# Four graph layers on a sparse matrix: moving a check of the matrix from layer 0 to layer 2, and the transposed writes to another queue

## The chip, the core and the metric

The kernel runs on one core of a Trainium2 chip. The metric is the device time of one execution in microseconds (us). Engines are named as in the profile: PE is the matrix engine (PEld its weight loads), DVE the vector engine, ACT the scalar engine, POOL the general one, SP the engine that here only issues transfers. A name with a q (SPq, ACTq) is an engine's instruction queue where it issues transfers. Each engine takes its instructions in order; engines wait for each other by semaphores.

## The reference

`x` is 2708 x 128 and `adj` 2708 x 2708, mostly zeros (some 16 entries in a row, all positive in the inputs, diagonal included). Four layers follow each other, each on the rectified layer norm `h` of `x`, each added to `x`. Cut to what matters:

```
layer 0:  x += (adj.T @ h) / adj.sum(axis=0)
layer 1:  m[i, j] = gelu(s[i] + d[j] + msg_b)            # s, d: two projections of h
          agg[i] = sum over j of m[i, j] * adj[i, j]
          u = gelu([h, agg] @ upd_w.T + upd_b) + h
          x += layer_norm(u) * ln_w + ln_b
layer 2:  msg = relu((adj @ h) @ W_msg.T + b_msg)
          x += gru_cell(msg, h)
layer 3:  for two heads: softmax over the mask (adj > 0 or diagonal) of
          leaky_relu(s_src[i] + s_dst[j]), times the head's values, + norm, elu
```

## The kernel before, in words

Rows and columns are cut into tiles of 128: 21 whole tiles and a tail of 20 (`NT` = 22, `TAIL` = 20). Six groups of up to four tiles are `GROUPS`: groups 0 to 4 have four tiles, group 5 two, one of them the tail. A chunk of columns is one group wide, up to 512.

**Layer 0** goes over items `(c, s)`: column chunk c of `adj`, row group s. For c from 0 to 4 the items run in order; the last chunk (`LAST` = 5) has its six pieces `z` loaded while c = 3 runs and worked between the items of c = 4. Loads go through SP's queue into `a`, a ring of four buffers (`RING`), so that the load of an item goes out three items ahead. For an item:

- DVE lists the largest eight values of each block of 124 columns in a row and their positions (`list_cut`, lines 348 and 350). Layer 1 works on these lists instead of on the whole matrix. Blocks that hold the diagonal are first copied by POOL with the diagonal taken out (`mask_near`).
- PE transposes the 4 x 4 blocks of the item into `p_T` (two PSUM banks, line 383), ACT copies each bank to `aT` (line 387), and SP writes `aT` to `adjT` in device memory (line 388), for layer 2. Each bank holds four transposes.
- Between the transposes PE multiplies the item with `h0` (line 369), into sums over the rows; a column of ones gives the degree. For c = 0 the products stand after all four transposes, since h0 is still being made by ACT (`sum_rows`, `sum_squares`, `normal_rows`), one group an item.
- ACT takes the sign of the item and adds it up into `total` (line 399, and 403 for the tail), and, where c = s, adds up the diagonal into `own`.

When a chunk's sums are complete, the items of the next chunk carry its further work: `invert` (DVE, s = 0), `spread` (ACT, POOL, s = 1), `sum_rows`, `sum_squares`, `normal_rows`, `turn_rows` (s = 5: PE transposes rows of h to `p_h`, ACT copies to `hT`), and one chunk later `destinations` and `split_destinations`. The order of all instructions is written out by hand (`manual_schedule`).

**Layer 1** opens with a list of single steps for the first row tiles: `count_rows`, `rank`, `select_rows` and so on. Among them stand the lists of the last column chunk, `list_last(n)` for the 22 row tiles, which read `z`. Then 23 periods work through the row tiles, with POOL, DVE and ACT preparing what PE multiplies. At its end DVE compares `total` with the number of listed entries and the signs of the diagonal; a difference, or a list or row that is too full, sets `flag`, and then a second, dense program runs after this one. With the given inputs it does not run.

**Layer 2** goes over six chunks of rows. `aggregate` loads a chunk of `adjT` in five pieces of up to five tiles, each piece to one of three buffers `a2` (SP, line 1247); the last piece has one whole tile and the tail of 20. DVE and POOL derive the mask from a piece (lines 1251 and 1254), PE multiplies it with h into `p_agg` (line 1259). `finish_chunk` is what follows for a chunk; its steps lie between the products of the next chunk, at distances counted in units of PE's work: ACT copies `aggc` and `hc` (1270, 151), PE and ACT make `msg` (1282), the gates (1294, 1295) and `nn`, DVE makes `y`, then come the layer norms for layer 3 (`h` and `z`, both line 136), `z3T` (1336), the `hv` products, `own_e` (1357), PE's `p_row` (1363), `own_T`, and two small transfers from ACT's queue for `row` (1370).

**Layer 3** weighs and multiplies the mask's rows (lines 1090 and 1120). It is not touched.

Of the kernel before, what the change touches and what calls it, by code (L numbers as in the profile page):

```python
# [20 lines left out]
F32 = mybir.dt.float32  # L21
BF16 = mybir.dt.bfloat16
AF = mybir.ActivationFunctionType
ALU = mybir.AluOpType
# [6 lines left out]
P = 128  # L31
# [29 lines left out]
def listed_layers(ctx: ExitStack, tc: tile.TileContext, x, adj, w, out, flag):  # L61
# [79 lines left out]
    def span(t, k):  # L141

        return t * P, min(k * P, N - t * P)
# [12 lines left out]
    val = keep.tile([P, NT, NB, S], F32, name="val")  # L156
    col = keep.tile([P, NT, NB, S], U16, name="col")
    own = keep.tile([P, NT], F32, name="own")
    total = keep.tile([P, len(GROUPS) + 1, len(GROUPS)], F32, name="total")
    nc.gpsimd.memset(total, 0.0)  # L160
    nc.gpsimd.memset(own, 0.0)
    inv = keep.tile([P, NT], F32, name="inv_deg")

# [118 lines left out]
    once0 = l0.enter_context(tc.tile_pool(name="l0h", bufs=1))  # L282
    pool = l0.enter_context(tc.tile_pool(name="l0k", bufs=2))
    marked = l0.enter_context(tc.tile_pool(name="l0n", bufs=8))
    turned = l0.enter_context(tc.tile_pool(name="l0t", bufs=7))
    sump = l0.enter_context(tc.tile_pool(name="l0p", bufs=4, space=PSUM))
    turnp = l0.enter_context(tc.tile_pool(name="l0q", bufs=2, space=PSUM))
    h0 = once0.tile([P, NT, D + 1], F32, name="h0")
# [47 lines left out]
    def list_cut(c, s, n):  # L336
# [9 lines left out]
        for k in range(0, len(units), 2):  # L346
            for b, v in units[k : k + 2]:
                nc.vector.max(val[0:m, n, b, :], v)  # L348
            for b, v in units[k : k + 2]:
                nc.vector.max_index(col[0:m, n, b, :], val[0:m, n, b, :], v)  # L350

    def work_cut(c, s):

        g0, gk = GROUPS[s]
        t0, tk = GROUPS[c]
        i0, iw = span(g0, gk)
        lo = window(c)[0]
        a = cuts[c, s]
        if s == 0:
            accs[c] = [  # L360
                sump.tile([P, CH], F32, name="sums")[:, 0 : 2 * (D + 1)].rearrange("p (q d) -> p q d", q=2)
                for _ in range(0, tk, 2)
            ]

        def products(n):
            m = size(n)
            for q in range(tk):
                k, e = size(t0 + q), (t0 + q) * P - lo
                nc.tensor.matmul(  # L369
                    accs[c][q // 2][0:k, q % 2, :], a[0:m, n - g0, e : e + k], h0[0:m, n, :],  # L370
                    start=(n == 0 and q % 2 == 0), stop=(n == NT - 1), skip_group_check=True,
                )

        todo = list(range(g0, g0 + gk))
        js = list(range(t0, t0 + tk))
        turns = [js[q : q + 2] for q in range(0, tk, 2)] if gk < 4 == tk else [[j] for j in js]
        for js in turns:
            p = turnp.tile([P, CH], F32, name="p_T")
            k, n = size(js[0]), len(js)
            for i, j in enumerate(js):  # L380
                for q in range(gk):
                    m, e = size(g0 + q), j * P - lo
                    nc.tensor.transpose(  # L383
                        p[0:k, i * iw + q * P : i * iw + q * P + m], a[0:m, q, e : e + k], ident[0:m, 0:m]
                    )
            aT = turned.tile([P, CH], F32, name="aT")
            nc.scalar.copy(aT[0:k, 0 : n * iw], p[0:k, 0 : n * iw])  # L387
            nc.sync.dma_start(
                adjT[0:k, js[0] : js[0] + n, i0 : i0 + iw], aT[0:k, 0 : n * iw].rearrange("p (j i) -> p j i", j=n)
            )  # L390
            if c > 0 and todo and gk == 4:
                products(todo.pop(0))
        for n in todo:
            products(n)

        e0, e1 = t0 * P - lo, t0 * P - lo + span(t0, tk)[1]
        whole = gk if gk == 4 else gk - 1
        sign = pool.tile([P, 4, CH], BF16, name="sign")
        nc.scalar.activation(
            sign[:, 0:whole, 0 : e1 - e0], a[:, 0:whole, e0:e1], AF.Sign, accum_out=total[:, s, c : c + 1]  # L400
        )
        if whole < gk:
            nc.scalar.activation(
                sign[0:TAIL, whole, 0 : e1 - e0], a[0:TAIL, whole, e0:e1], AF.Sign,
                accum_out=total[0:TAIL, s + 1, c : c + 1],
            )
# [62 lines left out]
    for i, (c, s) in enumerate(order):  # L469
# [5 lines left out]
            )  # L475
        for n in range(g0 + 1, g0 + gk):
            list_cut(c, s, n)
        if c > 0 and s == 0:
            invert(c - 1)
        if i + 1 < len(order):  # L480
            mask_near(*order[i + 1])
# [8 lines left out]
        if c == 0:  # L490
            for stage, g in (
# [5 lines left out]
                (),  # L497
            )[s]:
                stage(h0, *GROUPS[g]) if stage is normal_rows else stage(*GROUPS[g])
        elif s == 1:  # L500
            spread(c - 1)
        elif s == 2:
            sum_rows(*GROUPS[c - 1])
        elif s == 3:
            sum_squares(*GROUPS[c - 1])
        elif s == 4:
            normal_rows(h, *GROUPS[c - 1])
        elif s == 5:
            turn_rows(c - 1)
        if c > 1 and s == 0:  # L510
            destinations(c - 2)
        if c > 1 and s == 2:
            split_destinations(c - 2)
        if c == LAST - 1 and s > 0:
            work_cut(LAST, s - 1)
# [6 lines left out]
        if (c, s) == (2, 3):  # L522
# [5 lines left out]
            nc.gpsimd.tensor_copy(src_self[:, 0, :], msg_wT[:, 0, :])  # L528
            nc.gpsimd.tensor_tensor(src_self[:, 1, :], msg_wT[:, 0, :], msg_wT[:, 1, :], ALU.add)

    enter(LAST - 1)
    destinations(LAST - 2)
    work_cut(LAST, LAST)
    for q, k in ((0, P), (1, TAIL)):
        nc.scalar.copy(last_sums[0:k, q, :], accs[LAST][0][0:k, q, :])
    for s in range(len(GROUPS)):
# [26 lines left out]
    with (  # L563
# [408 lines left out]
            for k in range(1, GB):  # L972
                put_more(t, k)

        def list_last(n):
            list_cut(LAST, n // 4, n)
# [8 lines left out]

        puts = ExitStack()
        for step, n in (
            (list_last, 0), (count_rows, 0), (rank, 0), (list_last, 1), (select_rows, 0), (describe, 0), (rows, 4),
            (list_last, 2), (list_last, 3), (count_next, 0), (turn_rows, 4), (split_destinations, 3),
            (finish_rows, 0), (fetch_both, 0), (rank, 1), (destinations, 4), (enter, 5), (place, 0), (pass_on, 0),  # L990
            (sources, 0), (select_rows, 1), (split_destinations, 4), (rows, 5), (describe, 1),
            *((list_last, n) for n in range(4, 10)), (columns, 0), (turn_rows, 5), (destinations, 5),
            (finish_rows, 1), (fetch_both, 1), (rank, 2), (split_destinations, 5), (place, 1), (select_rows, 2),
            *((list_last, n) for n in range(10, 16)), (describe, 2), *((list_last, n) for n in range(16, NT)),
            (close_lists, 0),
        ):
            step(n)
# [4 lines left out]
        if True:  # L1002
# [6 lines left out]
        puts.close()  # L1009


        SETS = len(GROUPS) + 1
        lost = fix.tile([P, 4, NT], F32, name="lost1")
        nc.vector.reduce_sum(lost[:, 0, :], rows_n, AX.X)
        nc.vector.tensor_scalar(lost[:, 1, :], own, 0.0, None, ALU.is_gt)
        nc.vector.tensor_scalar(lost[:, 2, :], own, 0.0, None, ALU.is_lt)
        nc.vector.tensor_tensor(lost[:, 0, :], lost[:, 0, :], lost[:, 1, :], ALU.add)
        nc.vector.tensor_tensor(lost[:, 0, :], lost[:, 0, :], lost[:, 2, :], ALU.subtract)
        found, there = lost[:, 1, 0:SETS], lost[:, 2, 0:SETS]
        nc.vector.reduce_sum(  # L1020
            found[:, 0 : SETS - 2], lost[:, 0, 0 : NT - 2].rearrange("p (s t) -> p s t", t=4), AX.X
        )
        nc.vector.tensor_copy(found[:, SETS - 2 : SETS], lost[:, 0, NT - 2 : NT])
        nc.vector.reduce_sum(there, total, AX.X)
        nc.vector.tensor_tensor(there, there, found, ALU.not_equal)
        nc.vector.reduce_sum(flag, there, AX.X)
        over = fix.tile([P, 2], F32, name="over1")
        many = once.tile([P, NT, NB], BF16, tag="picked", name="many")
        nc.vector.tensor_tensor(many, ends, rows_n, ALU.add)
# [4 lines left out]
        for q in range(2):  # L1034
            nc.vector.tensor_tensor(flag, flag, over[:, q : q + 1], ALU.add)
    lists.close()


# [15 lines left out]
    ident_8 = l3.tile([P, P], U8, name="ident_8")  # L1054
    nc.vector.tensor_copy(ident_8, ident)
    PIECE = 5
    RUNS = ((0, 3), (3, 8), (11, 8), (19, 3))
    MOST = 8
    accs = ctx.enter_context(tc.tile_pool(name="l23p", bufs=1, space=PSUM))
# [174 lines left out]
    with (  # L1234
# [6 lines left out]
        def aggregate(t0, k0, pa, j0):  # L1241
# [5 lines left out]
            nc.sync.dma_start(a[:, 0:whole, 0:n], adjT[:, j0 : j0 + whole, c : c + n])  # L1247
            if whole < jn:
                nc.sync.dma_start(a[0:TAIL, whole, 0:n], adjT[0:TAIL, NT - 1, c : c + n])
            most = min(whole, PIECE - 1)  # L1250
            nc.vector.tensor_scalar(mask[:, j0 : j0 + most, c : c + n], a[:, 0:most, 0:n], 0.0, None, ALU.is_gt)
            if most < jn:
# [12 lines left out]
        def finish_chunk(t0, k0, pa):  # L1265
# [95 lines left out]
            yield 2  # L1361
            p = bank("p_row")
            nc.tensor.transpose(p[0 : 2 * k0, 0:P], own_e[:, 0 : 2 * k0], ident)
            turned = zpool.tile([8, P], F32, name="own_T")
            nc.scalar.copy(turned[0 : 2 * k0, :], p[0 : 2 * k0, 0:P])
            passed = wdram.tile([8, P], F32, name="own_d")
            nc.scalar.dma_start(passed[0 : 2 * k0, :], turned[0 : 2 * k0, :])
# [23 lines left out]
    nc.vector.tensor_scalar(wide[:, 1, :], sv, -LIMIT, None, ALU.is_lt)  # L1391
    over = out_pool.tile([P, 1], F32, name="over3")
    nc.vector.reduce_sum(over, wide, AX.XY)
    nc.vector.tensor_tensor(flag, flag, over, ALU.add)

    for q in range(5):
# [477 lines left out]
```

## Time and profile before

| | |
|---|---|
| median of 3 runs | 1079.67 us (1075.68 to 1081.86) |
| profiled execution: its time | 1080.01 us |
| its span | 1078.2 us |
| mean granted PE clock | 0.94 |
| busy PE, PEld, DVE | 934.4, 816.0, 795.4 us |
| busy ACT, POOL | 516.6, 471.0 us |
| moved by DMA | 133.64 MB |

The profile is of one execution. Busy times are sums over the span; stages with different limits lie behind them, so the tables by stretch say more. Issuing a transfer isn't counted as busy. "Idle before" an instruction names what ended the wait; a wait for several semaphores is put down to the one that came last.

### The profile page before, as it was taken

How to read it: one execution, taken by the hardware profiler on the slowest of the kernel's cores; microseconds unless marked ns; L12 is line 12 of the kernel's file. 1: busy time of each engine (PE TensorE's matmuls, PEld its weight loads, DVE VectorE, ACT ScalarE, POOL GpSimd, SP SyncE). 2: the span in 40 equal slices, each digit the busy share in tenths (PEclk: the TensorE clock that was granted, in tenths of full speed). 3: DMA queues.
4: the chain of work that ended last, by engine and by line, in shares of the span. 5: the costliest groups of instructions: out<-in, count | busy, mean ns of one | idle time of the engine just before them, and what ended most of it. 6: DMA issues, size and time to landing. Idle time of an engine off the chain costs nothing. (4 is left out here: it accounts for less than half of the span.)

```text
span 1078.2 us, 23412 instructions
## 1 busy us (share of the span) xinstructions
PE 934.4 (87%) x8632; PEld 816.0 (76%) x8632; DVE 795.4 (74%) x2748; ACT 516.6 (48%) x1427; POOL 471.0 (44%) x596
## 2 busy tenths in 40 slices
PE   3789878893399999999969978999988999999983
PEld 3789778772399999999969943444477899989982
DVE  7789978717877778897848264566668987898693
ACT  5968858664266666676646622333332200240142
POOL 6322221222397777898958354444311210250042
PEclk9899999985599999999989978999989999999996
DMA  8599899622133333333132045666410000000000
GB/s 286 183 337 299 257 364 346 224 91 84 50 100 124 123 119 97 118 98 113 62 108 83 29 147 206 206 224 212 138 37 2 27 9 1 2 16 6 2 11 19
DMA packets 77090, 133.64 MB, mean 124 GB/s; under 512 B 13980, under 2 KB 29456, under 8 KB 76966
## 3 DMA queue, kind: packets, MB, share of 16 engines
q1 hardware_dynamic: 75150, 129.26, 36.1%
q10 hardware_dynamic: 1816, 2.80, 0.8%
q8 instruction: 70, 1.15, 0.4%
q14 instruction: 54, 0.44, 0.1%
HBM read 85.41 MB, written 30.87 MB: 108 GB/s over the span
## 5 line engine op out<-in xcount | busy, mean ns | idle before, releaser
L721 POOL TENSOR_SCALAR put<-count,line,value 128x128 f32<-128x128 f32 x176 | 198.5, 1138 | 44.6 <-DVE value L710 30.7
L1120 PE MATMUL att<-hv,wt 128*128 128x129 f32 x1672 | 194.4, 277 | 8.7 <-DVE wt L1090 8.7
L1120 PEld LDWEIGHTS att<-hv,wt 128*128 128x128 f32 x1672 | 190.8, 193 | 11.6 <-DVE wt L1090 8.6
L807 PE MATMUL p_m<-d,cols 124*128 124x128 bf16 (+1 forms) x1452 | 163.5, 221 | 7.9 <-DVE cols L752 7.9
L803 PE MATMUL p_m<-s,sel 128*128 128x128 bf16 x1452 | 163.0, 221 | 7.4 <-ACT g L815 7.4
L1090 DVE SCALAR_TENSOR_TENSOR wt<-row,lift,mask 128x1024 f32<-128x1024 f32 (+1 forms) x132 | 138.7, 1082 | 23.2 <-PE att L1120 23.2
L120 POOL TENSOR_TENSOR n_r<-n_r,minus_half 128x4 f32<-128x4 f32 (+1 forms) x27 | 39.0, 1446 | 255.6 <-DVE n_r L119 251.9
L828 PE MATMUL agg<-put,g 128*128 128x128 f32 (+1 forms) x968 | 122.5, 278 | 0.0
L1259 PE MATMUL p_agg<-a,hs 128*128 128x512 f32 (+2 forms) x264 | 112.0, 567 | 10.7 <-issue 6.0
L369 PE MATMUL sums<-h,a 128*128 128x129 f32 (+1 forms) x880 | 121.2, 286 | 0.0
L828 PEld LDWEIGHTS agg<-put,g 128*128 128x128 f32 x968 | 113.2, 192 | 0.0
L369 PEld LDWEIGHTS sums<-h,a 128*128 128x128 f32 (+1 forms) x880 | 112.3, 202 | 0.9 <-issue 0.2
L383 PE MATMUL p_T<-ident,a 128*128 128x128 f32 (+1 forms) x440 | 74.1, 291 | 44.3 <-ACT aT L387 38.0
L803 PEld LDWEIGHTS <-sel 128*128 128x128 bf16 x1452 | 104.6, 98 | 9.2 <-issue 8.7
L807 PEld LDWEIGHTS <-cols 124*128 124x128 bf16 (+1 forms) x1452 | 103.8, 99 | 8.2 <-DVE cols L752 8.2
L730 ACT ACTIVATE put<-mine,value 128x128 f32<-128x128 bf16 x308 | 100.5, 391 | 0.0
L815 ACT ACTIVATE g<-p_m 128x512 f32<-128x512 f32 x132 | 72.6, 551 | 54.7 <-PE agg L828 42.3
L383 PEld LDWEIGHTS p_T<-ident,a 128*128 128x128 f32 (+1 forms) x440 | 54.8, 148 | 53.3 <-ACT aT L387 42.2
L1259 PEld LDWEIGHTS p_agg<-a,hs 128*128 128x128 f32 (+1 forms) x264 | 48.6, 198 | 60.9 <-issue 54.1
L350 DVE FIND_INDEX8 col<-val,a 128x8 uint16<-128x124 f32 x342 | 91.6, 279 | 0.0
L387 ACT COPY aT<-p_T 128x512 f32<-128x512 f32 (+2 forms) x122 | 66.1, 563 | 51.4 <-PE p_T L383 31.0
L348 DVE MAX8 val<-a 128x8 f32<-128x124 f32 x342 | 78.9, 271 | 10.5 <-DMA a<-in_adj 10.5
(282 smaller groups left out, 1559.8 us busy)
## 6 DMA issues: line engine op xcount, KB each, us to landing
adjT<-aT SPq DMA_DIRECT2D x105, 256.0 KB
a<-adjT SPq DMA_DIRECT2D x20, 1280.0 KB
spread<-passed SPq DMA_DIRECT2D x22, 704.0 KB
later<-sel SPq DMA_DIRECT2D x22, 616.0 KB
a<-in_adj SPq DMA_DIRECT2D x5, 1152.0 KB
a<-in_adj SPq DMA_DIRECT2D x5, 1120.0 KB
a<-in_adj SPq DMA_DIRECT2D x5, 1088.0 KB
a<-in_adj SPq DMA_DIRECT2D x5, 1056.0 KB
```

What stands on the lines that cost most here:

```text
L348: nc.vector.max(val[0:m, n, b, :], v)
L350: nc.vector.max_index(col[0:m, n, b, :], val[0:m, n, b, :], v)
L369: nc.tensor.matmul(accs[c][q // 2][0:k, q % 2, :], a[0:m, n - g0, e : e + k], h0[0:m, n, :], start=(n == 0 and q % 2 == 0), stop=(n == NT ...
L383: nc.tensor.transpose(p[0:k, i * iw + q * P : i * iw + q * P + m], a[0:m, q, e : e + k], ident[0:m, 0:m])
L721: nc.gpsimd.tensor_scalar(st["put", 0][:, b, :], count, st["line"][:, b : b + 1], st["value"][:, b : b + 1], ALU.is_equal, ALU.mult,)
L730: nc.scalar.activation(st["put", 1][:, b - HP, :], st["mine"][:, b - HP, :], AF.Identity, scale=st["value"][:, b : b + 1])
L803: nc.tensor.matmul(p[:, b - b0, :], st["sel"][:, b, :], s3[:, q, t % 2, :], start=(q == 0), stop=False)
L807: nc.tensor.matmul(p[:, b - b0, :], st["cols"][0:kb, b, :], d3[0:kb, b, q, :], start=False, stop=(q == 2))
L828: nc.tensor.matmul(agg, g[:, b - 4 * k, :], put, start=(b == 0), stop=False)
L1090: nc.vector.scalar_tensor_tensor(wt[:, 0:n], row[:, k, c : c + n], lift[:, j, k : k + 1], mask[:, j, c : c + n], op0=ALU.max, op1=ALU.mult,)
L1120: nc.tensor.matmul(banks[s // 3][:, s % 3, :], wt[:, q * P : (q + 1) * P], hv[:, j, k, :], start=(v < 2 and s // 3 not in touched), stop=( ...
L1259: nc.tensor.matmul(pa[:, 0:n], h[0:k, j, :], a[0:k, j - j0, 0:n], start=(j == 0), stop=(j == NT - 1))
```

## The change

1. The signs (lines 399 and 403), their sums `total` and the comparison at the end of layer 1 are taken out.
2. In layer 2 ACT adds up the negative parts of each piece of `a2` into `below`, one or two tiles to an instruction; a sum above zero sets `flag`.
3. The writes of `aT` are issued from ACT's queue, each after the next copy. `aT` has eleven buffers instead of seven.
4. For chunks 0 to 2, the work on a chunk's complete sums (`invert`, `spread` and what follows) begins one item later; `turn_rows` moves to s = 0 of the chunk after, `destinations` and `split_destinations` one item on, and for chunk 3 `turn_rows` stands after `enter(4)`.
5. Four `list_last` stand before `enter(4)`; the others close up in layer 1's opening.
6. `own_T` is taken from another pool.

```diff
-    total = keep.tile([P, len(GROUPS) + 1, len(GROUPS)], F32, name="total")
-    nc.gpsimd.memset(total, 0.0)
...
-    turned = l0.enter_context(tc.tile_pool(name="l0t", bufs=7))
+    turned = l0.enter_context(tc.tile_pool(name="l0t", bufs=11))
...
+    written = []
+    def write_one():
+        if written:
+            nc.scalar.dma_start(*written.pop())
...
             nc.scalar.copy(aT[0:k, 0 : n * iw], p[0:k, 0 : n * iw])
-            nc.sync.dma_start(
+            write_one()
+            written.append((
                 adjT[0:k, js[0] : js[0] + n, i0 : i0 + iw], aT[0:k, 0 : n * iw].rearrange("p (j i) -> p j i", j=n)
-            )
+            ))
...
-        nc.scalar.activation(
-            sign[:, 0:whole, 0 : e1 - e0], a[:, 0:whole, e0:e1], AF.Sign, accum_out=total[:, s, c : c + 1]
-        )
...
-        if c > 0 and s == 0:
+        off = 1 if c < LAST - 1 else 0
+        if c > 0 and s == off:
             invert(c - 1)
...
-        elif s == 1:
+        elif s == 1 + off:
             spread(c - 1)
-        elif s == 2:
+        elif s == 2 + off:
             sum_rows(*GROUPS[c - 1])
-        elif s == 3:
+        elif s == 3 + off:
             sum_squares(*GROUPS[c - 1])
-        elif s == 4:
+        elif s == 4 + off:
             normal_rows(h, *GROUPS[c - 1])
-        elif s == 5:
-            turn_rows(c - 1)
         if c > 1 and s == 0:
+            turn_rows(c - 2)
+        if c > 1 and s == 1:
             destinations(c - 2)
-        if c > 1 and s == 2:
+        if c > 1 and s == 3:
             split_destinations(c - 2)
...
+    for n in range(4):
+        list_last(n)
     enter(LAST - 1)
+    turn_rows(LAST - 2)
     destinations(LAST - 2)
     work_cut(LAST, LAST)
+    write_one()
...
-        nc.vector.reduce_sum(there, total, AX.X)
-        nc.vector.tensor_tensor(there, there, found, ALU.not_equal)
-        nc.vector.reduce_sum(flag, there, AX.X)
...
+    below = l3.tile([P, 3 * len(GROUPS) * ((NT + PIECE - 1) // PIECE)], F32, name="below")
+    nc.gpsimd.memset(below, 0.0)
+    looked = []
...
+            for m, q0, q1 in ((P, 0, min(2, whole)), (P, 2, min(4, whole)), (P, 4, whole), (TAIL, whole, jn)):
+                if q1 > q0:
+                    junk = pool.tile([P, 2, CH], U8, name="junk2")
+                    i = len(looked)
+                    looked.append(i)
+                    nc.scalar.activation(
+                        junk[0:m, 0 : q1 - q0, 0:n], a[0:m, q0:q1, 0:n], AF.Relu, scale=-1.0,
+                        accum_out=below[0:m, i : i + 1],
+                    )
...
-            turned = zpool.tile([8, P], F32, name="own_T")
+            turned = pool.tile([8, P], F32, name="own_T")
...
+    nc.vector.tensor_scalar(below, below, 0.0, None, ALU.is_gt)
+    nc.vector.reduce_sum(over, below, AX.X)
     nc.vector.tensor_tensor(flag, flag, over, ALU.add)
```

More of the change, by code (lines that the diff above doesn't have):

```diff
@@ L394, in work_cut @@
             products(n)
[L396 to L399, printed above, removed]
-            sign[:, 0:whole, 0 : e1 - e0], a[:, 0:whole, e0:e1], AF.Sign, accum_out=total[:, s, c : c + 1]
-        )
[L402 to L406, printed above, removed]
         if c == s:
@@ L529, in listed_layers, with list_last @@
             nc.gpsimd.tensor_tensor(src_self[:, 1, :], msg_wT[:, 0, :], msg_wT[:, 1, :], ALU.add)
+    def list_last(n):
+        list_cut(LAST, n // 4, n)
+    for n in range(4):
+        list_last(n)
     enter(LAST - 1)
+    turn_rows(LAST - 2)
     destinations(LAST - 2)
     work_cut(LAST, LAST)
+    write_one()
     for q, k in ((0, P), (1, TAIL)):
@@ L973, in put_rest @@
                 put_more(t, k)
-        def list_last(n):
-            list_cut(LAST, n // 4, n)
         def count_next(_):
@@ L987, in listed_layers @@
         for step, n in (
-            (list_last, 0), (count_rows, 0), (rank, 0), (list_last, 1), (select_rows, 0), (describe, 0), (rows, 4),
-            (list_last, 2), (list_last, 3), (count_next, 0), (turn_rows, 4), (split_destinations, 3),
+            (count_rows, 0), (rank, 0), (list_last, 4), (select_rows, 0), (describe, 0), (rows, 4),
+            (list_last, 5), (list_last, 6), (count_next, 0), (turn_rows, 4), (split_destinations, 3),
             (finish_rows, 0), (fetch_both, 0), (rank, 1), (destinations, 4), (enter, 5), (place, 0), (pass_on, 0),
             (sources, 0), (select_rows, 1), (split_destinations, 4), (rows, 5), (describe, 1),
-            *((list_last, n) for n in range(4, 10)), (columns, 0), (turn_rows, 5), (destinations, 5),
+            *((list_last, n) for n in range(7, 12)), (columns, 0), (turn_rows, 5), (destinations, 5),
             (finish_rows, 1), (fetch_both, 1), (rank, 2), (split_destinations, 5), (place, 1), (select_rows, 2),
-            *((list_last, n) for n in range(10, 16)), (describe, 2), *((list_last, n) for n in range(16, NT)),
+            *((list_last, n) for n in range(12, 17)), (describe, 2), *((list_last, n) for n in range(17, NT)),
             (close_lists, 0),
@@ L1009, in listed_layers @@
         puts.close()
[L1012 to L1023, printed above, removed]
-        nc.vector.reduce_sum(there, total, AX.X)
-        nc.vector.tensor_tensor(there, there, found, ALU.not_equal)
-        nc.vector.reduce_sum(flag, there, AX.X)
         over = fix.tile([P, 2], F32, name="over1")
@@ L1033, in listed_layers @@
         nc.vector.reduce_sum(over[:, 1:2], many, AX.XY)
-        for q in range(2):
-            nc.vector.tensor_tensor(flag, flag, over[:, q : q + 1], ALU.add)
+        nc.vector.tensor_tensor(flag, over[:, 0:1], over[:, 1:2], ALU.add)
     lists.close()
@@ L1393, in listed_layers @@
     nc.vector.reduce_sum(over, wide, AX.XY)
+    nc.vector.tensor_tensor(flag, flag, over, ALU.add)
+    nc.vector.tensor_scalar(below, below, 0.0, None, ALU.is_gt)
+    nc.vector.reduce_sum(over, below, AX.X)
     nc.vector.tensor_tensor(flag, flag, over, ALU.add)
```

## The prediction

> **What bounds the kernel now.** The table of windows comes first (columns: stretch in us, its length, busy us with instruction counts of PE, PEld, DVE, ACT, POOL, then granted clock, DMA share, GB/s). Layer 0 is 0 to 245, the opening of layer 1 245 to 293, its steady part runs to 627, layer 2 to 800, layer 3 to the end.
>
> ```profile
> 0.00:60.00 60.00, 37.17 (x259) 34.00 (x260) 44.85 (x294) 45.23 (x138) 25.04 (x83) 0.91 0.72 240
> 60.00:200.00 140.00, 117.92 (x957) 110.76 (x956) 125.78 (x833) 101.57 (x234) 33.91 (x92) 0.96 0.95 321
> 200.00:245.00 45.00, 42.73 (x289) 33.91 (x287) 13.08 (x80) 30.17 (x82) 12.80 (x38) 0.89 0.32 113
> 245.00:293.00 48.00, 14.27 (x120) 11.11 (x121) 42.60 (x180) 17.09 (x53) 12.86 (x20) 0.55 0.18 60
> 627.00:663.00 36.00, 25.56 (x49) 10.42 (x48) 20.21 (x65) 6.68 (x17) 22.56 (x18) 0.74 0.57 194
> 663.00:800.00 137.00, 132.50 (x403) 66.95 (x403) 85.32 (x238) 46.36 (x130) 51.85 (x33) 0.98 0.53 175
> ```
>
> Up to 60 nothing is full; from 60 to 200 DMA (0.95), DVE (0.90) and PE (0.84) are all near their ends; from 200 to 245 PE works off a backlog alone. From 245 to 293 DVE bounds, from 663 to 800 PE, with ACT two thirds idle. Then the list of waits up to 245 (us in total, times, longest), of PE and of SP's queue:
>
> ```profile
> PE p_T L383 <- ACT aT L387: 38.0, 17, 6.8
> PE p_T L383 <- DMA a<-in_adj: 6.2, 4, 4.6
> PE sums L369 <- ACT part_x L436: 2.9, 1, 2.9
> ```
> ```profile
> SPq L388 <- ACT aT L387: 95.7, 79, 7.2
> ```
>
> PE transposes into two p_T banks that ACT empties (L387). While ACT is inside a sign or a row sum, both fill and PE stands; SP, in order, stands at the write of aT (L388) behind the same copy, with the next load of adj behind it. The ACT timeline gives the prices (start, duration; idle before in brackets):
>
> ```profile
> 103.50 1.91 ACT L399 ACTIVATE sign<-a 128x2048 bf16<-128x2048 f32 x1
> ...
> 105.40 0.57 ACT L237 CAST d<-p_d 124x512 bf16<-124x512 f32 x1
> ...
> 712.13 0.49 ACT L136 ACTIVATE h<-xs,n_r 128x128 f32<-128x128 f32 x1 [5.58 <-DVE n_r L130]
> 712.20 0.36 ACTq L1370 DMA_DIRECT2D row<-own_d  x1
> 712.53 0.48 ACT L136 ACTIVATE h<-xs,n_r 128x128 f32<-128x128 f32 x1
> ```
>
> A sign holds ACT 1.90 us from start to start, its accumulator read included. A DMA issued between two activations costs ACT next to nothing: h follows h 0.40 us later with the issue, 0.41 without (four in 1.65).
>
> **What the Trainium skill says.** "ScalarE: Activation LUTs", What ACT_TABLE_LOAD costs: 186 ns plus 0.833 ns per element per partition with immediate scale and bias, neighbours overlapping by about 93. For 2048 that is 1892; the trace has 1914. "DMA: Bandwidth & Descriptors", Issuing engines are not separate DMA queues: transfers from SP and ACT share the same 16 engines, so a second queue saves issue time only. The trace has 320 ns (median) per write issue on SP; it can't show the sharing, since ACT moves only 2.80 MB. "Perfetto Trace Analysis", Per-instruction lifecycle: a DMA's semaphore wait is on the issuing sequencer. SP's 95.7 us agree; on ACT the instructions behind would then wait too.
>
> **The change, part by part.**
>
> *Signs out of layer 0.* 25 signs of 128x2048 (1.91), 5 of 512 (0.62) with 5 tail pieces (0.61), 6 on the last chunk (5 near 0.69, one 0.32): 48 + 6 + 4 = 58 us of ACT's 177 up to 245. Up to 60 they are 5 x 1.91 + 1.2 = 10.8 us, in a stretch where ACT runs solid from 13.8 to 57 and PE waits 16.7 of its 38 us (five waits, 5.49 to 0.90). DVE needs 44.9 us there and starts near 5, so the stretch can't end before 50: gain **10**. Behind it PE has 117.9 + 42.7 = 160.7 us of work, DMA (0.95 x 140 + 0.32 x 45) = 147, DVE 139. PE now takes 185, of which some 21 are waits on aT. If the aT waits go, PE is next at 161, with DMA 14 behind it; since loads must land ahead of PE, I leave 8 us of waits on loads: 169, gain **16**. Layer 0 together: 26. Bounds: with loads holding PE as much as ACT did, only the first 10 to 12; with nothing held, 10 + 24 + some of the modelled slack, 38.
>
> *Writes on ACT's queue, one copy late, eleven aT buffers.* 122 issues leave SP and go to ACT; at 0.3 to 0.4 us each they fit under the 0.58 us of the copy that was just started, and the copy they wait for is the one before: 0. The cover would go if ACT waited at the issue itself. The instruction order shows each write also waiting for an earlier DMA of its semaphore, eight DMAs back, at times a load. SP now waits 9.0 + 4.7 us for this at L388 (waits on loads and on writes); on ACT it stands ahead of the next aT copy, hence of PE. ACT's present 13.7 us of waits for a free aT buffer (seven buffers) should shrink by about as much. Taken as 0, from -10 to +14. Loads on SP pass the writes and need only a free ring buffer.
>
> *Sums one item later, turn_rows and destinations later.* DVE waits 30.2 us for sums, 19.0 of them the last, uncovered only by PE's end. The other 11 lie beside a DMA-bound stretch: counted in the 16. At the end p_h, hT and p_d now follow each other without transposes between: about +1 us of PE, in the 169's slack.
>
> *Four list_last ahead of enter(4).* Each is 0.87 us of DVE (249.34 to 250.20); one was already in DVE's 19 us gap, so three leave the DVE-bound opening: **-2.6**, taken as **-2**.
>
> *Flag arithmetic at the end of layer 1.* Some ten DVE operations of 0.15 to 0.35 us, beside a PE that is busy 317 of 334 us: 0. One memset and three small reductions added: 0, off the chain; exposed, 1 us. Other names and pools: 0.
>
> *Negative parts in layer 2.* Per piece of five tiles two 128x1024 and one 128x512. From signs of 2048 (1.91) and 512 (0.62) the slope is 0.84 ns, so 1.05 and 0.62: 2.72 a piece, 1.24 for the last piece, 12.1 a chunk, 66 us in all with the narrow chunk's 5.4. ACT has some 9.5 us of work in a chunk of 29, so it fits; what counts is its order. Two places:
>
> ```profile
> 652.38 0.88 ACT L136 ACTIVATE hs<-xs,n_r 128x128 f32<-128x128 f32 x2 [10.03 <-DVE n_r L130]
> ```
> ```profile
> 653.64 9.19 PE L1259 MATMUL p_agg<-a,hs 128*128 128x512 f32 x14 [4.42 <-DMA a<-adjT]
> ```
>
> First, the opening. Three buffers hold pieces 0 to 2; piece 3 is issued at 647.86, when POOL's mask frees piece 0, and PE starts on it at 653.64. In the new order the third sum of piece 0 stands behind this hs, so piece 0 comes free at 653.26 + 0.62 = 653.9: piece 3 is 6 us later, PE too: **+6**, and 1 more for a clock that is low after the longer gap.
>
> ```profile
> 748.91 0.56 ACT L1270 COPY aggc<-p_agg 128x512 f32<-128x512 f32 x1
> 749.38 0.58 ACT L151 COPY hc<-p_h 128x512 f32<-128x512 f32 x1
> 750.64 0.78 ACT L1336 ACTIVATE z3T<-p_z,b,g 128x512 f32<-128x512 f32 x1 [0.69 <-PE p_z L149]
> 751.50 0.69 ACT L1282 ACTIVATE msg<-p_m,b_msg 128x512 f32<-128x512 f32 x1
> ```
> ```profile
> 753.88 1.88 PE L1294 MATMUL p_rz<-msg,W_ihT 128*128 128x512 f32 x4
> ```
>
> Second, each chunk's end. z ends at 749.0; the last piece's 1.24 makes aggc 750.1 and hc end its slot at 751.1, piece 0's 2.72 makes z3T 753.8, msg ends at 755.2, and PE's L1294 moves from 753.88 by 1.3. The same steps at 664, 690, 719 and 778 give 0, 1.7, 0.7 and 0.3: **+4**. In two chunks own_e stands behind piece 1's 2.72 with 1.9 of slack (own_e ends at 704.1, PE's p_row starts at 706.0): 2 x 0.9, **+2**. Behind msg wait half_n, the gates and nn, then DVE's y; they move with it and are counted once. Layer 2: **+13**, from +5 (the opening's load lands early) to +40.
>
> Sum: -26 - 2 + 13 = **-15**. The profiled execution took 1080.0 (span 1078.2 and 1.8 around it), 0.3 above the median of 1079.67: 1065 against either.
>
> **The rivals.** *Loads hold layer 0.* DMA share 0.95 speaks for it: only the first 10 and 2 more, -12 - 2 + 13 = -1, 1079. Against: after 200 its share is 0.32, so it has time that PE's backlog leaves unused. *Layer 2 is nearly free and layer 0 gives more:* -32 - 2 + 6 gives 1052; for it, ACT's two thirds idle and PE's 38 us. *Slower: the sums stand at the head of ACT's queue.* If each chunk exposes its pieces 0 and 1 and the last one (2.72 + 2.72 + 1.24 = 6.7) instead of 1.2, layer 2 costs 5 x 6.7 + 7 = 40: -26 - 2 + 40 = +12, 1092. It decides from (28 - 7) / 5 = 4.2 us a chunk. Against: p_agg work of 19 us a chunk lies between PE's needs of ACT. *It doesn't do what it says:* the issues on ACT bring back in waits what the signs gave (+14 and more), which gives 1079 again and is in the first rival's chance.
>
> **How the numbers follow.** Forecast 0.55, loads hold 0.17, cheap layer 2 0.15, sums at the head 0.13. About 0.5% (5.4 us) is what a measurement of this kernel can tell from no change. Faster: 0.54 + 0.15 + 0.03 = 0.72; same 0.13, nearly all from the loads; slower 0.15, the sums and a worse case of the loads. The forecast's own range is 1056 to 1076 (layer 0 by 6, layer 2 by 5). The whole range, down past the 1052 and up to half way between 1079 and 1092: 1048 to 1086.
>
> **What would show it.** In the changed profile: PE's waits on aT under 10 us in sum; its work of layer 0 ending near 219, with a DMA share of 0.95 or more from 50 to about 195; ACT issues of 0.3 to 0.5 us, and waits of aT copies and of write issues for DMA of about 14 us in sum; PE starting on piece 3 some 32 us after layer 2's first load is issued (now 653.6 - 627.6 = 26); and the stretch from PE's last p_u to its first att product, now 627.5 to 796.8, near 182. The forecast is wrong if layer 0 ends after 232 or that stretch grows by over 20.

## The result, and the profile after

The changed kernel takes 1069.8 us (median of ten runs, 1068.2 to 1072.1), the kernel before 1077.84 beside it (1073.9 to 1081.9): a ratio of 0.992, 95% interval 0.991 to 0.994. The forecast was 1065, with 1048 to 1086 as its range; the time came out 5 us above it. The profiled execution spans 1070.3 us against 1078.2. By stage, from the places named in the prediction, the 7.9 us are made of −20.7 in layer 0, −3.9 in layer 1, **+13.9** in layer 2 (last p_u to first att) and +2.9 in layer 3. Layer 0 is taken to end where PE starts its first product of layer 1 (before, then changed):

```profile
244.76 0.19 PE L643 MATMUL p_r<-rows_n,before 128*128 128x22 bf16 x1
224.05 0.18 PE L645 MATMUL p_r<-rows_n,before 128*128 128x22 bf16 x1
```

The windows of the changed kernel, with the columns of the prediction's table:

```profile
0.00:60.00 60.00, 40.20 (x271) 36.67 (x272) 49.44 (x325) 35.09 (x126) 29.35 (x97) 0.94 0.80 259
60.00:200.00 140.00, 129.45 (x1069) 121.85 (x1068) 130.93 (x873) 74.41 (x207) 33.92 (x93) 0.98 0.94 329
200.00:245.00 45.00, 30.08 (x204) 21.75 (x203) 23.29 (x84) 20.47 (x57) 13.85 (x29) 0.81 0.27 92
627.00:663.00 36.00, 25.91 (x63) 11.64 (x64) 14.32 (x37) 25.27 (x51) 9.68 (x7) 0.81 0.56 191
663.00:800.00 137.00, 125.10 (x412) 66.43 (x411) 82.58 (x241) 93.24 (x254) 50.65 (x33) 0.98 0.47 152
```

ACT's column tells where the work went: 10 us less up to 60, 27 less from 60 to 200, 47 more from 663 to 800. PE did 12 matmuls more up to 60 and 112 more from 60 to 200, the work that before was left over for the stretch behind 200.

The waits up to 245 (us in total, times, longest), of PE, of ACT and of SP's queue:

```profile
PE p_T L387 <- ACT aT L391: 23.9, 14, 5.1
PE p_T L387 <- DMA a<-in_adj: 6.5, 4, 4.6
```
```profile
ACT aT L391 <- PE p_T L387: 47.6, 61, 4.5
ACT aT L391 <- DMA a<-in_adj: 19.0, 7, 5.7
ACT aT L391 <- DMA z<-in_adj: 4.3, 2, 3.1
```
```profile
SPq L306 <- PE sums L373: 50.8, 14, 6.4
SPq L312 <- PE sums L373: 24.2, 5, 9.2
```

PE's waits on aT fell from 38.0 to 23.9 and no further. The reason is in the second fence: a copy of aT reads p_T, a bank of PSUM, and yet it waits 19.0 us for loads of adj and 4.3 for loads of z. It reads neither; it stands in order behind a write whose issue waits for them. SP's 95.7 us at the writes are gone, but its loads now wait 75 us for PE to give back a ring buffer: most of that queue's wait has only changed its name. The last load of adj was issued at 181.1, 17.7 us sooner than before (198.8), but that is not the freed queue's doing: with the writes back on SP it was issued at 180.8 (e2 below). A piece of ACT's timeline (start, duration; idle before, and what ended it):

```profile
117.68 0.57 ACT L391 COPY aT<-p_T 128x512 f32<-128x512 f32 x1
119.74 0.33 ACTq L354 DMA_DIRECT2D adjT<-aT  x1
120.11 0.59 ACT L391 COPY aT<-p_T 128x512 f32<-128x512 f32 x1 [1.85 <-DMA b_msg<-in_b_msg]
121.13 0.33 ACTq L354 DMA_DIRECT2D adjT<-aT  x1
121.56 0.59 ACT L391 COPY aT<-p_T 128x512 f32<-128x512 f32 x1 [0.86 <-DMA ff<-in_ff]
123.55 0.33 ACTq L354 DMA_DIRECT2D adjT<-aT  x1
123.92 0.59 ACT L391 COPY aT<-p_T 128x512 f32<-128x512 f32 x1 [1.78 <-DMA attn<-in_attn]
```

Three writes in a row wait for small weights (SP had issued their loads 2 to 8 us earlier), and the copy behind each waits with it.

Layer 2's opening on ACT and on PE, and PE's waits from 645 to 786:

```profile
628.72 0.88 ACT L136 ACTIVATE hs<-xs,n_r 128x128 f32<-128x128 f32 x2 [5.33 <-DVE n_r L130]
629.50 0.61 ACT L1241 ACTIVATE junk<-a 128x512 uint8<-128x512 f32 x1
630.02 0.19 ACT L1241 ACTIVATION_READ_ACCUMULATOR junk<-a 128x1 f32 x1
630.24 1.06 ACT L1241 ACTIVATE junk<-a 128x1024 uint8<-128x1024 f32 x1
631.20 0.19 ACT L1241 ACTIVATION_READ_ACCUMULATOR junk<-a 128x1 f32 x1
631.42 1.06 ACT L1241 ACTIVATE junk<-a 128x1024 uint8<-128x1024 f32 x1
...
633.35 1.06 ACT L1241 ACTIVATE junk<-a 128x1024 uint8<-128x1024 f32 x1
```
```profile
636.90 8.42 PE L1254 MATMUL p_agg<-a,hs 128*128 128x512 f32 x14 [12.61 <-DMA a<-adjT]
```
```profile
PE p_m L1275 <- ACT hc L151: 1.8, 2, 1.0
PE p_row L1358 <- ACT own_e L1352: 1.7, 2, 0.9
PE p_rz L1289 <- ACT msg L1277: 1.1, 2, 0.5
```

The third sum of piece 0 stands behind hs, as the instruction order had it, so piece 3 comes late: PE's wait ahead of it is 12.61 us, it was 4.42. The start of one piece's sums to the next is 3.11 us (630.24 to 633.35), where the forecast had 2.72. At the ends of chunks the three waits that were foretold, on hc, own_e and msg, are there.

### The profile page after: what moved, and what is told of

Its sections match the earlier page's. It is cut to its first block, busy times and chain, and to the rows that moved or that the text cites. A ratio compares the mean times of both kernels' runs of the same rounds, so it can differ in the third digit from the quotient of the medians.

```text
span 1070.3 us, 23391 instructions
## 1 busy us (share of the span) xinstructions
PE 932.0 (87%) x8632; PEld 815.0 (76%) x8632; DVE 791.3 (74%) x2740; ACT 531.7 (50%) x1511; POOL 473.3 (44%) x596
## 5 line engine op out<-in xcount | busy, mean ns | idle before, releaser
L723 POOL TENSOR_SCALAR put<-count,line,value 128x128 f32<-128x128 f32 x176 | 202.1, 1161 | 40.3 <-DVE value L712 27.1
L387 PE MATMUL p_T<-ident,a 128*128 128x128 f32 (+1 forms) x440 | 72.6, 286 | 30.4 <-ACT aT L391 23.9
```

What stands on the lines that cost most here:

```text
L387: nc.tensor.transpose(p[0:k, i * iw + q * P : i * iw + q * P + m], a[0:m, q, e : e + k], ident[0:m, 0:m])
L723: nc.gpsimd.tensor_scalar(st["put", 0][:, b, :], count, st["line"][:, b : b + 1], st["value"][:, b : b + 1], ALU.is_equal, ALU.mult,)
```

## The experiments

Each kernel's ratio is to runs of the kernel before beside it on the same chip (their medians were 1075.9 to 1078.4). "Column 1" is PE's first transpose of the second column of adj; "layer 0" ends with PE's first product of layer 1; "layer 2" is from the end of the last p_u to the first att; layer 3 from there to the end of the span. The last four columns are of the profiled execution.

| kernel | median us | ratio, 95% interval | column 1 | layer 0 | layer 2 | layer 3 |
|---|---|---|---|---|---|---|
| before | 1077.84 | 1 | 60.7 | 244.8 | 169.3 | 281.4 |
| changed | 1069.8 | 0.991 to 0.994 | 59.2 | 224.1 | 183.2 | 284.3 |
| e1 no sums in layer 2 | 1058.16 | 0.979 to 0.987 | 61.1 | 228.9 | 169.4 | 283.2 |
| e2 writes on SP | 1060.78 | 0.982 to 0.990 | 54.7 | 213.0 | 181.8 | 284.7 |
| e3 signs out alone | 1054.45 | 0.975 to 0.984 | 55.1 | 222.0 | 168.7 | 284.0 |
| e4 sums read early | 1069.11 | 0.991 to 0.996 | 61.3 | 223.6 | 183.9 | 282.7 |
| e5 pairs on ACT | 1063.37 | 0.984 to 0.991 | 58.2 | 219.1 | 182.5 | 281.6 |
| e6 SP, sums spread out | 1062.9 | 0.982 to 0.989 | 54.7 | 212.7 | 184.4 | 285.1 |
| e7 SP, seven buffers | 1066.87 | 0.986 to 0.993 | 53.9 | 221.2 | 182.7 | 285.5 |
| e9 SP, pairs, one sum late | 1066.52 | 0.984 to 0.993 | 55.1 | 221.8 | 180.6 | 282.7 |
| e10 SP, one sum at head | **1051.65** | 0.973 to 0.980 | 53.9 | 213.3 | 174.7 | 282.4 |
| e11 the same, sums held back | 1063.23 | 0.985 to 0.992 | 53.8 | 212.9 | 186.6 | 283.1 |
| e12 pairs on ACT, six doubles | 1066.0 | 0.985 to 0.992 | 58.5 | 220.1 | 181.7 | 283.3 |
| e14 e5, weights later | 1062.29 | 0.983 to 0.988 | 55.1 | 221.4 | 182.8 | 281.5 |

### The parts of layer 0: e3, e2, e7, e4

e3, from the kernel before: both sign activations, `total` and the count made of it are deleted, and with them the check; nothing takes its place.

> The kernel before with only the signs and the count made of them taken out (the check on lost entries is left out; the writes stay on SP, seven buffers, sums read where they were, nothing added in layer 2). Theory A, that the signs on ACT held PE: layer 0 ends near 226 to 230, time near 1062, the first item of column 1 starts near 51. Rival C, that the queue brought the gain: layer 0 ends at 238 or later, time near 1072. Rival D, that DMA holds the first 60 us anyway: the first item of column 1 starts at 58 or later, as it did in the changed kernel (59.2), whatever the queue.

Layer 0 ended at 222.0, 22.7 us sooner, and column 1 began at 55.1, 5.5 sooner: taking out the signs alone, with every write still on SP, brings more than the whole change does. That the freed queue brought the gain (rival C) is out, and so is D: DMA doesn't hold the first 60 us at 58. Layer 0 and the time were better than expected (by 4 and 8 us), but column 1 began 4 us later than the 51 that were expected.

e2, from the changed kernel:

```diff
-            nc.scalar.dma_start(*written.pop())
+            nc.sync.dma_start(*written.pop())
```

> The changed kernel with the writes of transposed rows issued on SP's queue again, still one copy late and with eleven buffers. Theory A, that ACT stands in layer 0 at write issues for DMAs eight back (about 30 us of DMA waits on ACT): these waits leave ACT, PE's waits on aT fall from 24 to under 12 us, but SP stands there and issues loads later; layer 0 ends between 215 and 232. Rival C, that the freed SP queue is what brought layer 0's gain: layer 0 ends at 238 or later (before 244.8, changed 224.1), time 1084 or more. Layer 2 as in the changed kernel (183).

One word moves layer 0 from 224.1 to 213.0 (215 to 232 was expected) and column 1 from 59.2 to 54.7. Among the waits of ACT's aT copies up to 230 there is no load left, only writes for whose buffers a copy waits. ACT's two longest waits, and PE's on aT:

```profile
ACT aT L391 <- PE p_T L387: 46.6, 61, 2.9
ACT aT L391 <- DMA adjT<-aT: 11.3, 11, 2.8
```
```profile
PE p_T L387 <- ACT aT L391: 16.5, 9, 5.1
```

PE's waits on aT were 16.5 us, not under 12: a part of them is not the queue's doing. e6, e10 and e11 have the same layer 0 and ended it at 212.7, 213.3 and 212.9. With writes on ACT, the same layer 0 ended at 224.1 and 228.9 in two kernels (changed, e1): that form is slower, and less steady in these two executions. A part of e1's 4.8 us can be the clock, whose mean over layer 0 was 0.94 in e1 and 0.97 in the changed kernel.

e7 is e2 with `bufs=7` for aT.

> The changed kernel with the writes on SP's queue and with seven aT buffers in place of eleven. With eleven, layer 0 ended at 213; with the signs out alone (seven buffers, written at once, sums read early) at 222, where ACT waited 26.8 us for aT buffers to be written out, against 11.3. Theory: the buffers make the difference; layer 0 ends at 218 to 224 and ACT waits over 20 us for buffers. Rival: it is the late write or the late reading; layer 0 ends at 212 to 216.

Layer 0 ended at 221.2. ACT's waits up to 230:

```profile
ACT aT L391 <- DMA adjT<-aT: 39.8, 19, 4.9
ACT aT L391 <- PE p_T L387: 31.1, 41, 2.4
```

The wait for a free buffer is 39.8 us in place of 11.3. Four buffers are worth 8.2 us of layer 0; with seven, the other parts of the change in layer 0 (writing late, reading sums late, four list_last ahead; e7 against e3) make a difference of 0.8. The medians go the same way: 1066.9 with seven, 1060.8 with eleven (e2).

e4, from the changed kernel: `off = 0`, turn_rows and the destinations as in the kernel before.

> The changed kernel with the sums read, the rows turned and the destinations made at the items where the kernel before had them (one item sooner). Theory A, that this part only fills gaps: layer 0 ends within 3 us of the changed kernel's 224, PE waits up to 3 us on part_x at some columns, time within 3 us of 1069.8. Rival: reading one item later carries 8 us or more of layer 0's gain, since DVE's wait for sums would hold the lists and with them the ring buffers: layer 0 ends at 232 or later, time 1077 or more.

Layer 0 ended at 223.6 and the time is within 1 us of the changed kernel's. This part of the change neither gives nor costs anything that these runs can tell.

### What ACT waits for at a write: e5, e12, e14

e5, from the changed kernel: one aT tile of 128x2x512, two copies into it, one write behind both (`bufs=5`).

```diff
-            aT = turned.tile([P, CH], F32, name="aT")
+            if not two or u % 2 == 0:
+                aT = turned.tile([P, 2, CH], F32, name="aT")
...
+            elif u % 2:
+                written.append((adjT[0:k, js[0] - 1 : js[0] + 1, i0 : i0 + iw], aT[0:k, :, 0:iw]))
```

> The changed kernel with two transposed blocks of 128x512 written by one DMA of 512 KB (61 to 65 write issues on ACT's queue in place of 122; five double aT buffers in place of eleven single ones). Theory A, that an ACT write stands for the DMA eight back, which is a load of SP's still on its way: with three DMAs an item in place of five, eight back is a load that has long landed, ACT's waits on loads of adj and weights in layer 0 fall from about 30 us to under 10, column 1 starts near 55 (changed 59.2, writes on SP 54.7), layer 0 ends near 213 to 217, time near 1060. Rival E, that what costs is the issue itself on ACT, or that ACT's queue takes the 16 engines away from the loads: only half of it or nothing comes back, column 1 starts at 57 or later, layer 0 ends at 219 or later, time 1065 or more.

Between the two. ACT's waits for loads up to 230 went from 30 to 12 us, near the 10 that A said, and from column 1 to the end layer 0 took 160.9 us (changed 164.8, e2 158.3). But column 1 still began at 58.2, and the median, 1063.4, lies between the two expectations. The timeline of ACT ahead of column 1 has one such wait:

```profile
48.02 1.07 ACT L393 COPY aT<-p_T 128x512 f32<-128x512 f32 x2 [1.52 <-DMA msg_wT<-in_msg_wT]
```

e12 is e5 with `bufs=6`.

> The changed kernel with paired writes on ACT's queue and six double buffers in place of five (sums in layer 2 as in the changed kernel). With five, ACT's waits on loads fell from about 30 to 12 us and layer 0 ended at 219. If buffers are what still holds it, layer 0 ends at 212 to 216 here, time near 1060; if the issue on ACT holds it (the wait for a load or the issue itself), it stays at 218 to 221, time near 1063.

With six double buffers layer 0 ended at 220.1: buffers don't hold the paired form on ACT. e14 moves what that copy waits for:

```diff
-        if (c, s) == (0, 3):
+        if (c, s) == (1, 3):
             nc.sync.dma_start(msg_wT, w["msg_wT"])
```

> The kernel with paired writes on ACT's queue (five double buffers), and the six weight loads that stood after the fourth item of column 0 put after the fourth item of column 1. With pairs alone, column 1 began at 58.2 and an aT copy at 48.0 had waited 1.5 us in ACT's queue for the weight msg_wT, which it doesn't read; with pairs on SP's queue column 1 began at 55.1. Theory A, that an ACT write stands for an earlier DMA of SP's: the wait at 48 goes, column 1 begins between 54.5 and 56, and such a wait turns up after 80 where the loads now are; layer 0 ends between 215 and 219, time 1060 to 1063. Rival E, that an issue on ACT costs by itself: column 1 begins at 58 as before, and layer 0 ends at 219 or later.

Column 1 began at 55.1, so the 3.1 us go with that wait. It was itself only 1.5 us; the granted clock, 0.62 from 48 to 52 behind it in e5, was 1.00 there in e14, and whether the wait brought the clock down isn't shown. ACT's timeline at the new place of the loads reads:

```profile
83.05 0.37 ACTq L354 DMA_DIRECT2D adjT<-aT  x1
83.46 1.07 ACT L393 COPY aT<-p_T 128x512 f32<-128x512 f32 x2 [5.51 <-DMA msg_wT<-in_msg_wT]
```

The wait went where the loads went and grew to 5.51 us, so that layer 0 as a whole gained nothing (221.4; 215 to 219 was expected). A write on ACT waits for a DMA that SP issued and that has nothing to do with it: the two queues are tied. That they are tied by semaphores which DMAs of both queues take in turn was read from the instruction order and isn't tested by itself. Rival E falls for the first column: each write's issue was still on ACT and took about 0.37 us there, and column 1 began as early as with pairs on SP (55.1, e9). Over the whole of layer 0 pairs don't settle it: it ended at 219 to 221 with them on ACT, at 222 with them on SP. The Trainium skill ("Perfetto Trace Analysis", Per-instruction lifecycle) has a DMA's semaphore wait on the issuing sequencer; these lines agree, and show what it costs when that sequencer also feeds an engine that others wait for.

### The order of the sums in layer 2: e1, e6, e9, e10, e11

e1, from the changed kernel: the loop of sums, `below` and its use are deleted.

> The changed kernel without layer 2's sums of negative parts (that check is left out; all else as changed). Theory A, that layer 2 pays for the sums by order on ACT: the stretch from PE's last p_u to its first att product goes from 183 back to about 169, PE starts on piece 3 about 8 us sooner, and the time is about 1056 (14 less than the changed kernel's 1069.8). Rival B, that part of the 14 us comes from the other buffers and from a later start in a low clock: the stretch stays over 174, time 1061 or more. Layer 0 ends near 224 in both. Layer 3 took 2.9 us more in the changed kernel: if it stays at 284 here, the sums don't cause it; if it returns to 281, they do.

Layer 2 took 169.4 us, within 0.2 of what it took before the change. The sums cost 13.7, and the moved own_T and the later start cost nothing in sum: rival B is out. (PE's wait ahead of piece 3 was 6.33, so that it began 6 us sooner and not 8.) From chunk 0's last product (p_w) on, the changed kernel needs 140.8 us to the first att, e1 133.6, the kernel before 134.0.

e6, from e2: the three sums are emitted one by one after the products of tiles 0, 1 and 2 of the piece.

> The changed kernel with the writes on SP's queue and with each piece's sums of negative parts not in one block ahead of the piece's products, but one after the products of each tile, so that steps of the chunk before (aggc, hc, msg, the gates) come between them. Theory A, that layer 2 pays 8 us at its opening, where piece 0's third sum stands behind hs on ACT in either order, and 6 us for the chunk's ends: the stretch from the last p_u to the first att goes from 182 (writes on SP) to 175 to 178, and its first idle stretch before piece 3 stays at 12.5. Rival F, that the 14 us are paid for ACT's load, not its order: the stretch stays at 181 or more.

A miss, and on the side of rival F by its own words: 184.4. The wait ahead of piece 3 was 10.74, but the part from p_w on was 143.7, 3 longer than with the sums in a block. e9, from e2 with pairs: one sum of 128x2560 a piece, after the first tile's products.

> The changed kernel with the paired writes on SP's queue, and in layer 2 one sum of 128x2560 a piece in place of three, emitted after the first tile's products (three wt buffers in place of four at the end of layer 2, to make room for the longer scratch tile). In its order on ACT the sum of piece 0 stands ahead of the last hs. Theory A: the wait before piece 3 goes from 12.5 back to about 6, a sum takes 2.3 us and a piece 2.5 in place of 3.1; the stretch from the last p_u to the first att is 170 to 173; layer 0 ends at 211 to 217; time near 1048. Rival F, load and not order: a stretch of 179 or more, time 1056 or more.

The opening did as expected, 5.78 us ahead of piece 3; the rest didn't, 144.7 from p_w on, and with 180.6 for the stretch this too fell to F. PE's longest waits from 637 to 782:

```profile
PE p_hv L1354 <- DVE hv L1360: 5.5, 3, 2.8
PE p_m L1290 <- ACT hc L151: 2.2, 4, 1.1
```

A sum now stands between the short activations that feed hv, which PE's p_hv waits for by way of DVE; in the changed kernel that wait is 0.4. And five double buffers on SP ended layer 0 at 221.8, with 19.6 us of waits for buffers: pairs give a buffer back late.

e10, from e2: one sum of 128x2560 a piece, at the head where the three stood; to make room, three wt buffers in place of four at the end of layer 2.

```diff
-            for m, q0, q1 in ((P, 0, min(2, whole)), (P, 2, min(4, whole)), (P, 4, whole), (TAIL, whole, jn)):
+            for m, q0, q1 in ((P, 0, whole), (TAIL, whole, jn)):
```

> The changed kernel with the writes on SP's queue, eleven single buffers, and one sum of 128x2560 a piece where the three sums stood, at the piece's head (three wt buffers in place of four). Theory A': the opening's 6.3 us come back as they did with one sum a piece after the first tile (wait before piece 3 about 6), and at the head of the pieces the sums do not get between the steps that feed hv, so the chunks' part stays at 139 to 141 (changed 140.8, without sums 133.6). Stretch from last p_u to first att 174 to 177, layer 0 ends at 213, time 1053 to 1056. Rival F, that longer sums hurt the chunks wherever they stand: chunks' part 144 or more, time 1059 or more.

1051.65 us, the lowest median of all, 2.4% under the kernel before, with the check kept (e1 and e3 leave theirs out). ACT's and PE's timelines at the opening:

```profile
613.47 2.34 ACT L1241 ACTIVATE junk<-a 128x2560 uint8<-128x2560 f32 x1 [3.63 <-POOL below L1041]
615.72 0.19 ACT L1241 ACTIVATION_READ_ACCUMULATOR junk<-a 128x1 f32 x1
620.18 0.88 ACT L136 ACTIVATE hs<-xs,n_r 128x128 f32<-128x128 f32 x2 [4.28 <-DVE n_r L130]
```
```profile
622.45 8.86 PE L1254 MATMUL p_agg<-a,hs 128*128 128x512 f32 x14 [5.40 <-DMA a<-adjT]
```

The sum of piece 0 is over 4.28 us before hs may start, and the wait ahead of piece 3 is 5.40 in place of 12.45 in e2. From p_w on it takes 138.3, against 140.7 in e2.

e11, from e10: the last piece's short sums and the next chunk's first sum wait until that chunk's third tile.

> As the one before (one sum at the head), but the last piece's two short sums and the next chunk's first sum are held back until the third tile of that chunk, behind aggc, hc, msg, the gates and nn. Theory A': PE's waits on hc and msg (changed: 1.8 and 1.1 us) go, those on own_e or hv may grow by as much since the sums only move; chunks' part 137 to 142, time 1051 to 1057. Rival F: 144 or more, as when the sums were spread (143.7).

Another miss, by more: from p_w on 149.0. PE's longest waits from 635 to 780:

```profile
PE p_agg L1262 <- DMA a<-adjT: 6.5, 3, 3.2
PE p_row L1371 <- ACT own_e L1365: 5.4, 2, 2.7
```

The waits on hc and msg went, as meant. But a sum that is late holds its piece's buffer, so loads come late (6.5 us), and two sums in a row ahead of own_e hold p_row. Order on ACT decides how much layer 2 pays: the same sums cost 5.4 us (e10) or 17.3 (e11) over 169.3. F, load and not order, can't explain that pair. That a lighter load helps as well isn't excluded: from e2 to e10 the sums kept their place and became one in place of three.

## Why the prediction was right, and where it was not

*Layer 0, forecast −26, measured −20.7.* The step that failed is "gain 10" up to 60: the changed kernel gained 1.4, and e1 and e4, whose layer 0 is the same up to there, began column 1 even 0.5 and 0.7 later than the kernel before (at a mean granted clock of 0.89 up to there, against 0.94 in the changed kernel). Two terms of it were mis-sized. Taking out the signs alone gives 5.5 (e3): the sum let PE's 16.7 us of waits on aT shrink until DVE bounds at 50, but without the signs PE still waited 10.3 us for aT in the first 55. And the writes on ACT take 4.5 back (59.2 against 54.7). The second half, "gain 16", came out at 19.3.

*Writes on ACT's queue, forecast 0 from −10 to +14.* About right as a sum, and wrong inside. From e3's 222.0 to the changed 224.1 is +2, made of −0.8 for the late write, the late reading and list_last, −8.2 for four more buffers and +11.1 for the queue; each is a difference of two profiled executions. The text named the mechanism, ACT standing for an earlier DMA of the same semaphore, but took over SP's 13.7 us for it; on ACT it was 30 (19.0 + 4.3 for adj and z, the rest for weights and at a row sum), because a held copy holds PE, PE then gives ring buffers back late and the loads, which the next writes wait for, are late in turn. That a held copy holds PE is shown. The rest of the chain is read from SP's 75 us of waits on sums and only argued, and it can't carry all 11 us: the first load of z was issued at 132.1 against 126.1 in e2, but the last load of adj at 181.1 against 180.8. The price of the issue itself was right, though the 0.41 of an h without it should have been 0.39 from start to start, (1.65 − 0.49) / 3.

*Sums one item later.* Counted as nothing of its own: right (e4).

*Layer 1, forecast −2 for list_last.* The opening gave 1.9; the steady part took another 2 us less, which no step foresaw. The whole of layer 1 differs by 3 us among the kernels that share it, so those 2 stay unexplained.

*Layer 2, forecast +13, measured +13.9.* Right in size, place and cause: +8.2 ahead of piece 3 (forecast 7), +6.8 at the chunks' ends (forecast 6), less 1.1 at other places of the opening. The waits on hc, own_e and msg are 4.6 of the 6.8; the rest isn't traced wait by wait. The price of a piece was 3.11 and not 2.72: one 128x1024 sum starts 1.18 us after the other, where the signs' slope said 1.05. Each sum starts only when the accumulator's read of the one before is over (in the opening's timeline above, the read from 631.20 to 631.39 and the next sum at 631.42). A read alone doesn't force that, for the row sums of layer 0 start beside it:

```profile
124.41 0.40 ACT L256 ACTIVATE junk<-xs,flat 128x128 f32<-128x128 f32 x1
124.72 0.19 ACT L256 ACTIVATION_READ_ACCUMULATOR junk<-xs,flat 128x1 f32 x1
124.81 0.39 ACT L256 ACTIVATE junk<-xs,flat 128x128 f32<-128x128 f32 x1
```

The row sums have two scratch buffers to write to, the sums of layer 2 one, which may be the cause; no run tried a second one.

*Layer 3, forecast 0, measured +2.9.* Over all kernels here layer 3 took 281.4 to 285.5, e3 without the sums 284.0 and e5 with them 281.6. So the 2.9 can't be put down to the change; the profiled execution of before was at the low end.

*The rivals.* Loads didn't hold layer 0 at 224: 11 us sooner was possible with the same loads (e2). Sums at the head of the queue cost 6.8 / 5 = 1.4 us a chunk, far from the 4.2 at which the sign would turn. "Doesn't do what it says" held in part: what the issue waits brought back, 11 us, is about half of what the signs gave. By the list of what would show it: PE's waits on aT (under 10 foretold, 23.9 measured) and ACT's waits for DMA (14 against 30) failed, and layer 0's end was 5 late. DMA's share from 50 to 195 was 0.95, as foretold; piece 3 began 34.0 us after the first load was issued (32 foretold), and the stretch of layer 2 was 183.2 (182). That the total came within 5 us is in part luck: 8.6 us less than forecast up to 60 stand against 3.3 more in layer 0's second half and 2 more in layer 1.

## What to carry to other kernels

Before a DMA is moved to a compute engine's queue, look at what its issue waits for beside its data: an engine that others wait for should not stand for another queue's loads. Here SP, with nothing else to do, was the better place for single writes, though its 95.7 us of waits made it look like the bottleneck. Work taken off one stage and put into another is priced by its order there: ask at each place who stands behind it on the engine, and which buffer it keeps. When parts of a change come out at zero together, run them apart: here four buffers and one queue were worth about −8 and +11.

## What the runs showed of the hardware

A write of aT on ACT's queue waited up to 5.51 us for a weight that SP was loading, though it shares no data with it (e14); with the writes on SP (e2), the waits of ACT's copies for loads were gone. The Trainium skill ("DMA: Bandwidth & Descriptors", Issuing engines are not separate DMA queues) says that a second issuing engine saves issue time only; here it saved none that counted and cost 11 us. A sum with its accumulator read came every 1.18 us at 128x1024 and every 2.44 at 128x2560 (620.97 to 623.41 in e10), against 1.06 and 2.32 for the activation alone, each with one scratch buffer: three short sums cost 0.67 us a piece more than one long one.
